# Layer 0 attention: finer side steps for channel attention and statistics, and a fifth buffer of weights in the second sample

## The chip, the cores and the metric

The kernel runs on one core of a Trainium2 chip. The metric is the device time of one launch in microseconds. Before the change it was measured in three runs: 4051.79, 4053.4 and 4055.28 us, so the median is 4053.4 us. One more execution was taken with the hardware profiler, and all durations of instructions come from it.

## What is computed

Two images x of 128 channels and 64 x 64 pixels go through four layers, each x = x + layer(groupnorm(x)). The change concerns layer 0 alone. Cut to what matters:

```python
xn = biasfree_ln(x, ln1_w)
qkv = conv1x1(xn, w_qkv)
qkv = depthwise_3x3(qkv, w_dw)                       # 5 groups of 128 channels
q1, k1, v, q2, k2 = split(qkv, 5)                    # 4 heads of 32 channels each
q1, q2, k1, k2 = map(l2norm_tokens, (q1, q2, k1, k2))
attn1 = softmax(einsum('bhnc,bhmc->bhnm', q1, k1) * temperature)   # 4096 x 4096 per head
out1 = einsum('bhnm,bhmc->bhnc', attn1, v)
attn2 = softmax(einsum('bhnc,bhnd->bhcd', q2, k2) * temperature)   # 32 x 32 per head
out2 = einsum('bhnc,bhcd->bhnd', v, attn2)
out = conv1x1(out1 + out2, w_po)
out = conv1x1(biasfree_ln(out, ln2_w), w_proj) + b_proj

def _gn(v, G=32, eps=1e-5):                          # before every layer
    m = mean(g); s = var(g)                          # over 4 channels and all pixels
    return (g - m) / sqrt(s + eps)
```

The first pair, attn1 and out1, is the token attention. The second, attn2 and out2, is called channel attention here.

## The kernel before

Layer 0 treats the two samples one after the other. For each it runs the convolutions (`convolutions`), then the attention (`attention`), and the end of the layer (`finish`), which is spread into the next sample's convolutions or runs by itself after the second sample.

`attention` is one loop of 256 iterations per sample, written out in full: 8 blocks of 512 queries (`qb`) times 32 tiles of 128 keys (`kt`). All four heads are treated in one iteration, on four groups of 32 rows of TensorE. Iteration n issues, in this order:

- the score matmuls of n (`scores`, L1850 in the profile): one head's scores into the single bank 6, three heads' into three of the banks 0 to 5, which alternate between even and odd iterations;
- the row-sum matmuls (`totals`, the same line L1842 as the multiplication), only at kt 28 and at kt 1;
- ScalarE's exponential of the single bank (L1918), a side step in every fourth iteration (n % 4 == 3), and the exponential of the three banks (L1921), both into the tile `weights` of n (128 x 4 x 512 f32, 8 KB in each partition);
- the multiplication of the weights of n-2 with the values (`multiply`, L1842), accumulated over a block;
- VectorE's addition of the weights of n (`add`, L1873, 128 x 2048), by which the row sums are collected in two interleaved series (even and odd n) and cut into shorter sums at the key tiles STARTS = (0, 1, 14, 27). At these four tiles nothing is added: the sum starts from the weights' own tile, which is then read by the addition two iterations later;
- after a row-sum matmul, ScalarE's copy of the bank to `total` (`emptied`, L1889), and in the first iterations of the next block the transposes, the reciprocal and the scaling of the block's queries by VectorE (`normalized`, L1895 to L1904, with the tile `turned`).

Inside `_in_order` every engine executes its instructions in the program's order, so an instruction that waits holds back all that follow on its engine. The tiles of `pool` (f0_p) have 4 buffers, except the three of `sums` and the single `total` and `turned`. The exponentials of iteration n overwrite the weights of n-4, so they wait for the last reader of those: TensorE's multiplication and VectorE's addition.

Side work hides beside this loop. It is written as generators, and `next(side)` runs one piece up to the next `yield`; a piece's instructions stand in the engines' queues before the second exponential and the addition of its iteration. Piece k is issued in iteration 4k-1. In the first sample `side` holds `channel_attention` (7 yields) and then `normalize` of the second sample (40 yields, among them the 11 of `_stats_steps`); in the second sample it holds `channel_attention` and `_stats_steps` for the first sample's output (the statistics that layer 1 needs). What is not done when the loop ends is run after it. PSUM for side pieces comes from `half()`, which takes one of the two banks that `at["spare"]` names: they belong to the other parity's three banks.

`channel_attention` folds the heads' products of q2 and k2 by two matmuls (L1781, 512 columns, and L1782, 8 columns, which needs the reduction L1779), copies them by ScalarE (L1786, L1788), reduces them per head (L1793, L1799), takes the norms' power -0.5 on GpSimd (`_power`, L1403 and L1404), scales, transposes and exponentiates a 128 x 32 tile (L1802 to L1810), divides (L1811, L1816) into the block-diagonal `a2`, transposes that (L1820) and multiplies it with `w_po` (L1826) into `w2`.

`xn`, the normalized input (128 x 4096 f32), is read by the convolutions. In the first sample, the second sample's `normalize` writes it anew during the attention. In the second sample nothing uses it after the convolutions.

Of the kernel before, what the change touches and what calls it, by code (L numbers as in the profile page):

```python
# [10 lines left out]
F32 = mybir.dt.float32  # L11
# [7 lines left out]
CH = 512  # L19
# [1381 lines left out]
def _power(nc, pool, out, x, least, add, exponent):  # L1401

    nc.vector.tensor_scalar(out, x, least, add, ALU.max, ALU.add)  # L1403
    nc.gpsimd.tensor_tensor(out, out, exponent.to_broadcast(list(out.shape)), ALU.pow)  # L1404


def _stats_steps(nc, pool, psum_tile, x, cst, mhalf, got, by_scalar=False):

    def taken(ps, name):
        if not by_scalar:  # L1410
            return ps[:, 0:1]
        t = pool.tile([128, 1], F32, tag=name, name=name)
        nc.scalar.copy(t, ps[:, 0:1])
        return t

    st = pool.tile([128, NCH, 6], F32, tag="gn_st", name="gn_st")
    for c in range(NCH):
        nc.vector.bn_stats(st[:, c, :], x[:, c * CH : (c + 1) * CH])
        yield
    mv = pool.tile([128, 2], F32, tag="gn_mv", name="gn_mv")  # L1420
    nc.vector.bn_aggr(mv, st)
    yield
    pm = psum_tile()
    nc.tensor.matmul(pm[:, 0:1], cst["group"], mv[:, 0:1], start=True, stop=True)
    mean = got[:, 0:1]
    nc.vector.tensor_copy(mean, taken(pm, "gn_pm"))
    d = pool.tile([128, 1], F32, tag="gn_d", name="gn_d")
    nc.vector.tensor_sub(d, mv[:, 0:1], mean)
    e = pool.tile([128, 1], F32, tag="gn_e", name="gn_e")
    nc.vector.scalar_tensor_tensor(e, d, d, mv[:, 1:2], ALU.mult, ALU.add)  # L1430
    yield
    pv = psum_tile()
    nc.tensor.matmul(pv[:, 0:1], cst["group"], e, start=True, stop=True)
    _power(nc, pool, got[:, 1:2], taken(pv, "gn_pv"), 0.0, 1e-5, mhalf)
    yield


# [11 lines left out]
def _layer0(ctx, tc, X, a, cst, worst, there, dram):  # L1449
    nc = tc.nc  # L1450
# [15 lines left out]
    def half():  # L1466
        if at["spare"] is None:
            return sp()[:, 0, :]
        return banks[:, at["spare"].pop(0), :]

    ident = cst["ident"]
    mhalf = one.tile([128, 1], F32, name="mhalf")
# [303 lines left out]
    def channel_attention(ss2, own, w2):  # L1776

        sums = small.tile([128, 2, 4], F32, tag="sums2", name="sums2")
        nc.vector.tensor_reduce(sums, ss2, AX.X, ALU.add)  # L1779
        ps, sq = half(), half()  # L1780
        nc.tensor.matmul(ps, fold.rearrange("p r i -> p (r i)"), own.rearrange("p r c -> p (r c)"), start=True, stop=True)  # L1781
        nc.tensor.matmul(  # L1782
            sq[:, :8], fold.rearrange("p r i -> p (r i)"), sums.rearrange("p n r -> p (n r)"), start=True, stop=True
        )
        folded = cp.tile([128, CH], F32, tag="gn", name="folded", bufs=1)
        nc.scalar.copy(folded, ps)  # L1786
        both = small.tile([128, 8], F32, tag="both", name="both")
        nc.scalar.copy(both, sq[:, :8])  # L1788
        gram = small.tile([128, 32], F32, tag="gram", name="gram")
        n2 = small.tile([128, 2], F32, tag="n2", name="n2")  # L1790
        for r in range(4):
            rr = slice(32 * r, 32 * r + 32)
            nc.vector.tensor_reduce(  # L1793
                gram[rr, :],
                folded[rr, r * 128 : (r + 1) * 128].rearrange("p (c q) -> p q c", c=4),
                AX.X,
                ALU.add,
            )
            nc.vector.tensor_copy(n2[rr, :], both[rr, r:8:4])  # L1799
        yield  # L1800
        _power(nc, small, n2, n2, 1e-24, 0.0, mhalf)
        nc.vector.tensor_scalar_mul(gram, gram, n2[:, 1:2])  # L1802
        lg = small.tile([128, 32], F32, tag="lg", name="lg")
        nc.vector.transpose(lg, gram)
        nc.vector.tensor_scalar(lg, lg, n2[:, 0:1], temp, ALU.mult, ALU.mult)
        nm = small.tile([128, 1], F32, tag="nm2", name="nm2")
        nc.vector.tensor_reduce(nm, lg, AX.X, ALU.max, negate=True)
        yield
        sm = small.tile([128, 1], F32, tag="sm2", name="sm2")
        nc.scalar.activation(lg, lg, AF.Exp, bias=nm, accum_out=sm)  # L1810
        nc.vector.reciprocal(sm, sm)  # L1811
        a2 = small.tile([128, 128], F32, tag="a2", name="a2", bufs=1)
        nc.gpsimd.memset(a2, 0.0)
        for h in range(4):
            hh = slice(32 * h, 32 * h + 32)
            nc.vector.tensor_scalar_mul(a2[hh, hh], lg[hh, :], sm[hh, :])  # L1816
        yield
        yield
        pt = half()
        nc.tensor.transpose(pt[:, :128], a2, ident)  # L1820
        a2t = small.tile([128, 128], F32, tag="a2t", name="a2t", bufs=1)
        nc.scalar.copy(a2t, pt[:, :128])
        yield
        yield
        pt = half()
        nc.tensor.matmul(pt[:, :128], a2t, w_po, start=True, stop=True)  # L1826
        nc.scalar.copy(w2, pt[:, :128])
        yield


    def attention(pool, side):

        sums = acc(1)
        single = banks[:, 6, :]
# [50 lines left out]
            return qb, first, bank  # L1885

        def emptied(qb, first, bank):
            t = pool.tile([128, CH], F32, tag="total", name="total", bufs=1)
            nc.scalar.copy(t, bank)  # L1889
            totalled.append((qb, first, t))  # L1890

        def normalized(qb, first, t):
            cols = slice(qb * CH, (qb + 1) * CH)
            turned = pool.tile([128, CH // 32, 32], F32, tag="turned", name="turned", bufs=1)
            nc.vector.transpose(turned.rearrange("p n i -> p (n i)"), t)  # L1895
            if first:
                by_query[qb] = small.tile([128, CH // 32], F32, tag="first", name="first")
                nc.vector.tensor_copy(by_query[qb], turned[:, :, 0])
                return
            rec = small.tile([128, CH // 32], F32, tag="rec", name="rec")  # L1900
            nc.vector.tensor_add(rec, turned[:, :, 0], by_query.pop(qb))
            nc.vector.reciprocal(rec, rec)
            nc.vector.transpose(turned, rec.unsqueeze(2).to_broadcast([128, CH // 32, 32]))
            nc.vector.tensor_mul(  # L1904
                q1[:, cols], q1[:, cols], turned.rearrange("p n i -> p (n i)")
            )

        for n in range(last + 1):
            kt = n % NQT
            mine, other = 3 * (n % 2), 3 * ((n + 1) % 2)  # L1910
            three = banks[:, mine : mine + 3, :]
            at["spare"] = [other, other + 1]
            held[n] = pool.tile([128, 4, CH], F32, tag="weights", name="weights")
            scores(n, three)
            total = None
            if len(pending) == 2 and kt in (STARTS[-1] + 1, 1):
                total = totals(banks[:, other + 2, :])
            nc.scalar.activation(held[n][:, 0, :], single, AF.Exp)  # L1918
            if n % 4 == 3:
                next(side, None)  # L1920
            nc.scalar.activation(held[n][:, 1:, :], three, AF.Exp)  # L1921
            if total:
                emptied(*total)
            if n > 1:
                multiply(n - 2)
            add(n)
            if totalled and kt < 2:
                normalized(*totalled.pop())
# [56 lines left out]
    def chain(*gens):  # L1985
        for g in gens:
            yield from g
# [31 lines left out]
    for b in range(B):  # L2019
        w2 = small.tile([128, 128], F32, tag="w2", name="w2")  # L2020
        with tc.tile_pool(name="f0_conv", reuse_waits="tile", bufs=1) as pool, _in_order(tc):
            ss2, own = convolutions(pool, b, before)
        if b == 0:

            with _after(tc):
                rows_of_weights = _weights_by_rows(nc, dram, a)
        side = [channel_attention(ss2, own, w2)]
        if b + 1 < B:
            side.append(normalize(b + 1))
        if b:  # L2030
            side.append(
                _stats_steps(
                    nc,
                    small,
                    half,
                    X[:, b - 1, :],
                    cst,
                    mhalf,
                    there[:, b - 1],
                    by_scalar=True,  # L2040
                )
            )
        with tc.tile_pool(name="f0_p", reuse_waits="tile", bufs=4) as pool, _in_order(tc):
            attention(pool, chain(*side))
        before = finish(b, w2)
    with _in_order(tc):
        run(before)
# [530 lines left out]
```

## Time and profile before

| | |
|---|---|
| median of three runs | 4053.4 us |
| profiled execution, its own time | 4055.79 us |
| its span, first to last instruction | 4054.0 us |
| TensorE busy in the span | 3872.8 us (96%) |
| VectorE busy | 3198.9 us (79%) |
| ScalarE busy | 3242.3 us (80%) |
| attention of the first sample | about 189 to 776 us |
| attention of the second sample | about 969 to 1536 us |
| TensorE, VectorE, ScalarE busy in 189 to 776 | 570.06, 541.99, 520.07 of 587 us |
| TensorE, VectorE, ScalarE busy in 969 to 1536 | 556.88, 527.66, 507.03 of 567 us |
| exponential L1918, L1921 (mean) | 0.599, 1.446 us |
| addition L1873 (mean) | 2.287 us |

A line of the timeline reads: start in us, duration in us, engine, line of the kernel, operation, output<-inputs, shapes, number of merged instructions, and in brackets the engine's idle time before it with what ended it. PE is TensorE, PEld its loading of weights, DVE is VectorE, ACT is ScalarE, POOL is GpSimd. A line of the page's group list ends with the busy time, the mean duration in ns, and the idle time of the engine just before, with what ended most of it. In the attention three engines are all busy for nine tenths of the time, so a short wait of one soon becomes a wait of another.

### The profile page before, as it was taken

To read this page: it belongs to the slowest core of one execution; us is meant where nothing else is said; L and a number is where in the kernel's file an instruction comes from. 1 tells how busy PE (TensorE), PEld (TensorE's weight loads), DVE (VectorE), ACT (ScalarE), POOL (GpSimd) and SP (SyncE) were. 2 spreads that over 40 slices of the span, in tenths; PEclk is the share of its full clock that TensorE was granted. 3 is DMA by queue.
4 is the path that set the end of the run, shared out by engine and by line. 5 is a ranking of instruction groups with operands and counts; after the bars stand their busy time and mean duration, and the time that the engine had idled before them with its cause. 6 is when DMAs were issued, how large, how long until landed. Compare 5 with 4: busy or idle time off the path is not lost.

```text
span 4054.0 us, 82178 instructions
## 1 busy us (share of the span) xinstructions
PE 3872.8 (96%) x35214; PEld 1324.0 (33%) x35214; DVE 3198.9 (79%) x3572; ACT 3242.3 (80%) x3955; POOL 90.7 (2%) x145
## 2 busy tenths in 40 slices
PE   7899999989999998997998999999999999999998
PEld 4511221244121114445665222232222322222222
DVE  5699999766999998996766787777777777776666
ACT  4489889735899993325654899999999999999998
POOL 1000000010010001000000000000000000000000
PEclk9999999999999998998998999999999999999999
DMA  1199960000000000003663110110002000110000
GB/s 50 17 197 187 185 105 2 1 2 2 2 2 2 2 2 13 6 1 150 278 259 112 53 40 27 45 55 27 27 29 73 25 27 30 39 52 6 6 6 4
DMA packets 193128, 217.59 MB, mean 54 GB/s; under 512 B 30441, under 2 KB 154345, under 8 KB 188658
## 3 DMA queue, kind: packets, MB, share of 16 engines
q1 hardware_dynamic: 192754, 212.25, 20.3%
q8 instruction: 278, 4.55, 0.5%
q14 instruction: 96, 0.79, 0.1%
HBM read 178.64 MB, written 98.57 MB: 68 GB/s over the span
## 4 chain that ended last, share of the span: by engine, by line
PE 65%; DVE 7%; ACT 2%; issue 2%; POOL 0%; SPq 0%; DMA 0%; ACTq 0%; POOLq 0%; DVEq 0%
PE ps_acc L2293 25%; PE ps_s L2270 18%; PE ps L1842 5%; PE ps L1850 5%; PE ps_bank L710 2%; DVE sums L1873 2%; PE ps_z L1008 2%; DVE e L950 2%; PE ps_t L640 1%; PE ps_bank L590 1%; PE ps_bank L681 1%; PE ps_bank L1062 1%; PE ps_acc L2151 1%; PE ps_acc L2197 1%; PE ps_pe L925 1%
## 5 line engine op out<-in xcount | busy, mean ns | idle before, releaser
L2284 ACT ACTIVATE weights<-ps_s 128x1024 f32<-128x1024 f32 x1920 | 1781.4, 1062 | 75.6 <-PE ps_s L2270 75.5
L2293 PE MATMUL ps_acc<-weights,vt 128*32 128x512 f32 x8192 | 1092.7, 605 | 0.0
L1873 DVE TENSOR_TENSOR sums<-sums,weights 128x2048 f32<-128x2048 f32 x384 | 855.3, 2287 | 15.8 <-ACT weights L1921 14.5
L2270 PE MATMUL ps_s<-q,k 64*128 64x512 f32 x4096 | 831.0, 470 | 3.7 <-DMA k<-stack 2.5
L1921 ACT ACTIVATE weights<-ps 128x1536 f32<-128x1536 f32 x512 | 740.6, 1446 | 8.9 <-PE ps L1850 8.9
L2270 PEld LDWEIGHTS ps_s<-q,k 64*128 64x128 f32 x4096 | 348.4, 184 | 935.7 <-ACT weights L2284 809.2
L1850 PE MATMUL ps<-q,k 32*64 32x512 f32 x8192 | 577.0, 615 | 21.6 <-ACT weights L1918 19.4
L1842 PE MATMUL ps<-weights,vt 128*32 128x512 f32 x4096 | 548.3, 607 | 0.0
L2242 DVE SCALAR_TENSOR_TENSOR exp_z<-exp_z,exp_m 128x1024 f32<-128x1024 f32 x384 | 469.1, 1222 | 9.3
L1918 ACT ACTIVATE weights<-ps 128x512 f32<-128x512 f32 x512 | 306.8, 599 | 107.1 <-DVE sums L1873 38.6
L2226 DVE TENSOR_SCALAR exp_i<-ps_s 128x1024 int32<-128x1024 f32 x128 | 156.8, 1225 | 216.2 <-PE ps_s L2270 216.0
L1850 PEld LDWEIGHTS ps<-q,k 32*64 32x64 f32 x8192 | 120.8, 130 | 456.4 <-ACT weights L1918 403.4
L2293 PEld LDWEIGHTS ps_acc<-weights,vt 128*32 128x32 f32 x8192 | 161.9, 108 | 309.3 <-issue 308.5
L1842 PEld LDWEIGHTS ps<-weights,vt 128*32 128x32 f32 x4096 | 84.4, 108 | 392.7 <-issue 379.4
L662 DVE SCALAR_TENSOR_TENSOR X<-g,w,X 128x2048 f32<-128x2048 f32 x84 | 197.4, 2351 | 2.6
L1873 DVE TENSOR_TENSOR sums<-weights 128x2048 f32<-128x2048 f32 x64 | 145.9, 2289 | 39.8 <-ACT weights L1921 39.3
L2246 DVE SCALAR_TENSOR_TENSOR weights<-exp_z,exp_i 128x1024 f32<-128x1024 f32 x128 | 156.8, 1225 | 15.9 <-ACT weights L2284 0.5
L2242 DVE SCALAR_TENSOR_TENSOR exp_z<-exp_m 128x1024 f32<-128x1024 f32 x128 | 156.0, 1219 | 0.0
L1008 PE MATMUL ps_z<-w_ri,e 128*32 128x128 f32 x2048 | 137.3, 408 | 14.1 <-DVE e L950 11.9
L1613 PE MATMUL ps<-pad,diag 32*32 32x512 f32 x4032 | 142.3, 604 | 4.1 <-ACT vt L1624 3.7
L1591 PE MATMUL ps<-xn,w_qkv 128*128 128x512 f32 (+1 forms) x200 | 87.3, 583 | 22.5 <-ACT pad L1598 14.1
L950 DVE TENSOR_SCALAR e<-ps_pe 32x136 f32<-32x136 f32 (+1 forms) x352 | 104.3, 296 | 4.9
(304 smaller groups left out, 2976.7 us busy)
## 6 DMA issues: line engine op xcount, KB each, us to landing
w_ri<-w_r SPq DMA_DIRECT2D x16, 2112.0 KB, 8.0
w_ri<-w_i SPq DMA_DIRECT2D x16, 2112.0 KB, 13.6
stack<-qs SPq DMA_DIRECT2D x64, 256.0 KB, 2.1
q<-stack SPq DMA_DIRECT2D x128, 128.0 KB, 2.5
k<-stack SPq DMA_DIRECT2D x128, 128.0 KB, 2.6
stack<-ks SPq DMA_DIRECT2D x32, 256.0 KB, 2.2
w_r<-in_L_conv_kr_w SPq DMA_DIRECT2D x15, 528.0 KB, 12.6
w_r<-in_L_conv_kr_x SPq DMA_DIRECT2D x15, 528.0 KB, 12.6
```

What stands on the lines that cost most here:

```text
L662: nc.vector.scalar_tensor_tensor(xi, g[:, i : i + H // 2, j : j + W], w8[:, s : s + 1], xi, ALU.mult, ALU.add)
L950: nc.vector.tensor_scalar_mul(out, got[of, :, s], sign)
L1008: nc.tensor.matmul(out.rearrange("p (n f o) -> p n f o", n=2, f=2), e[:, s, 2 * j : 2 * j + 2, :].rearrange("p f x -> p (f x)"), w.rearran ...
L1842: nc.tensor.matmul(out[rows, :], lhs(rows), w[:, j, :], start=first, stop=stop)
L1850: nc.tensor.matmul(bank[64 * h : 64 * h + 64, :], k1[rows, kt * 128 + 64 * h : kt * 128 + 64 * h + 64], q1[rows, qb * CH : (qb + 1) * CH], ...
L1873: nc.vector.tensor_add(parts[p].rearrange("p j c -> p (j c)"), t.rearrange("p j c -> p (j c)"), w.rearrange("p j c -> p (j c)"),)
L1918: nc.scalar.activation(held[n][:, 0, :], single, AF.Exp)
L1921: nc.scalar.activation(held[n][:, 1:, :], three, AF.Exp)
L2242: nc.vector.scalar_tensor_tensor(z, x, n, m, ALU.add, ALU.mult)
L2270: nc.tensor.matmul(ps[j // 2][:, j % 2, :], g.k[kt // 4][rows, j // 2, keys], g.q[qb][rows, j // 2, :], start=True, stop=True,)
L2284: nc.scalar.activation(w[0], ps[p], AF.Exp)
L2293: nc.tensor.matmul(g.ac[32 * j : 32 * j + 32, :], g.vt[:, kt, j // 2, i : i + 2, :].rearrange("p a d -> p (a d)"), w[:, i, :], start=(at = ...
```

## The change

There are two parts.

The first cuts side work into more pieces. In `channel_attention` the clearing of `a2` moves to the first piece, which otherwise keeps only the reduction L1779; a yield stands between this and the folding matmuls, one between ScalarE's copies of them and the reductions per head, one after `_power`, and one after the exponential. Two empty pieces go: the double yields before and after the transpose become single ones. It has 9 yields instead of 7. `_stats_steps` gets, for its use beside an attention (`by_scalar`), a yield after each of ScalarE's two copies out of PSUM, before VectorE reads the copy: 13 instead of 11. All that comes later in `side` is issued 2 or 4 pieces, that is 8 or 16 iterations, later.

The second part concerns the sample number b, which `attention` now gets. The tile `weights` has 4 + b buffers. In the second sample `total` and `turned` are not tiles of the pool but the first and the second 512 columns of `xn`. There is one of each, as before.

```diff
@@ _stats_steps
-    nc.vector.tensor_copy(mean, taken(pm, "gn_pm"))
+    got_mean = taken(pm, "gn_pm")
+    if by_scalar:
+        yield
+    nc.vector.tensor_copy(mean, got_mean)
...
-    _power(nc, pool, got[:, 1:2], taken(pv, "gn_pv"), 0.0, 1e-5, mhalf)
+    var = taken(pv, "gn_pv")
+    if by_scalar:
+        yield
+    _power(nc, pool, got[:, 1:2], var, 0.0, 1e-5, mhalf)
     yield
@@ channel_attention
         nc.vector.tensor_reduce(sums, ss2, AX.X, ALU.add)
+        a2 = small.tile([128, 128], F32, tag="a2", name="a2", bufs=1)
+        nc.gpsimd.memset(a2, 0.0)
+        yield
         ps, sq = half(), half()
...
         nc.scalar.copy(both, sq[:, :8])
+        yield
         gram = small.tile([128, 32], F32, tag="gram", name="gram")
...
         yield
         _power(nc, small, n2, n2, 1e-24, 0.0, mhalf)
+        yield
         nc.vector.tensor_scalar_mul(gram, gram, n2[:, 1:2])
...
         nc.scalar.activation(lg, lg, AF.Exp, bias=nm, accum_out=sm)
+        yield
         nc.vector.reciprocal(sm, sm)
-        a2 = small.tile([128, 128], F32, tag="a2", name="a2", bufs=1)
-        nc.gpsimd.memset(a2, 0.0)
         for h in range(4):
             hh = slice(32 * h, 32 * h + 32)
             nc.vector.tensor_scalar_mul(a2[hh, hh], lg[hh, :], sm[hh, :])
-        yield
         yield
         pt = half()
         nc.tensor.transpose(pt[:, :128], a2, ident)
...
         yield
-        yield
         pt = half()
@@ attention
-    def attention(pool, side):
+    def attention(pool, b, side):
...
-            t = pool.tile([128, CH], F32, tag="total", name="total", bufs=1)
+            t = xn[:, :CH]
+            if b == 0:
+                t = pool.tile([128, CH], F32, tag="total", name="total", bufs=1)
             nc.scalar.copy(t, bank)
...
-            turned = pool.tile([128, CH // 32, 32], F32, tag="turned", name="turned", bufs=1)
+            turned = xn[:, CH : 2 * CH].rearrange("p (n i) -> p n i", i=32)
+            if b == 0:
+                turned = pool.tile([128, CH // 32, 32], F32, tag="turned", name="turned", bufs=1)
...
-            held[n] = pool.tile([128, 4, CH], F32, tag="weights", name="weights")
+            held[n] = pool.tile([128, 4, CH], F32, tag="weights", name="weights", bufs=4 + b)
```

More of the change, by code (lines that the diff above doesn't have):

```diff
@@ L2043, in _layer0 @@
         with tc.tile_pool(name="f0_p", reuse_waits="tile", bufs=4) as pool, _in_order(tc):
-            attention(pool, chain(*side))
+            attention(pool, b, chain(*side))
         before = finish(b, w2)
```

## The prediction

> **What bounds the kernel now.** First the whole page, for the chain of waits and the costliest groups.
>
> ```profile
> ## 4 chain that ended last, share of the span: by engine, by line
> PE 65%; DVE 7%; ACT 2%; issue 2%; POOL 0%; SPq 0%; DMA 0%; ACTq 0%; POOLq 0%; DVEq 0%
> ...
> L1873 DVE TENSOR_TENSOR sums<-sums,weights 128x2048 f32<-128x2048 f32 x384 | 855.3, 2287 | 15.8 <-ACT weights L1921 14.5
> ...
> L1921 ACT ACTIVATE weights<-ps 128x1536 f32<-128x1536 f32 x512 | 740.6, 1446 | 8.9 <-PE ps L1850 8.9
> ...
> L1918 ACT ACTIVATE weights<-ps 128x512 f32<-128x512 f32 x512 | 306.8, 599 | 107.1 <-DVE sums L1873 38.6
> ```
>
> TensorE leads. In layer 0's attention (189 to 776 us for the first sample, 969 to 1536 for the second) ScalarE waits 38.6 us for VectorE's additions to free a buffer of weights. Then the timeline, undisturbed in the second sample:
>
> ```profile
> 1404.34 0.60 ACT L1918 ACTIVATE weights<-ps 128x512 f32<-128x512 f32 x1 [0.46 <-PE ps L1850]
> ...
> 1405.20 1.11 PE L1850 MATMUL ps<-q,k 32*64 32x512 f32 x16
> ...
> 1407.24 1.11 PE L1850 MATMUL ps<-q,k 32*64 32x512 f32 x16
> ...
> 1408.70 0.60 ACT L1918 ACTIVATE weights<-ps 128x512 f32<-128x512 f32 x1 [0.38 <-DVE sums L1873]
> ...
> 1409.35 1.12 PE L1850 MATMUL ps<-q,k 32*64 32x512 f32 x16
> ...
> 1410.72 4.49 DVE L1873 TENSOR_TENSOR sums<-sums,weights 128x2048 f32<-128x2048 f32 x2
> ```
>
> Score groups (L1850) normally start 2.04 us apart (1405.20 to 1407.24): I call this the beat. A late buffer moves the next start, 1409.35, to 2.11. And the worst place in the second sample's first block:
>
> ```profile
> 1005.36 1.11 PE L1850 MATMUL ps<-q,k 32*64 32x512 f32 x16
> ...
> 1007.03 0.60 ACT L1918 ACTIVATE weights<-ps 128x512 f32<-128x512 f32 x1 [0.65 <-DVE sums L1873]
> ...
> 1016.31 0.60 ACT L1918 ACTIVATE weights<-ps 128x512 f32<-128x512 f32 x1 [2.94 <-DVE sums L1873]
> ...
> 1016.96 1.50 PE L1850 MATMUL ps<-q,k 32*64 32x512 f32 x16 [2.76 <-ACT weights L1918]
> ...
> 1018.79 1.94 PE L1842 MATMUL ps<-weights,vt 128*32 128x512 f32 x8
> ```
>
> VectorE is late by a side step, ScalarE waits 2.94 us for its buffer, TensorE idles 2.76 us; afterwards the multiply takes 1.94 us instead of 1.06.
>
> **The skill.** "TensorE: Matmul & The Clock Gate", Part 1 (the HAM clock gate), says that an idle stretch puts TensorE at half clock for a window of about 3.4 us. The trace agrees: its clock record is 0.5 from 1017.57 to 1020.99 (3.42 us), and likewise from 201.79, 239.33 and 580.67 in the first sample. The same page (Architectural detail) calls ScalarE and VectorE strict FIFO: what stands behind a waiting instruction waits too, as the additions here do. "Perfetto Trace Analysis", Optimization Strategy, says that repeated equal bubbles can mean too few buffers; here ScalarE waits for a buffer four times in every undisturbed block.
>
> **The rule that I carry.** Let an iteration's score group start at P. From the timeline: L1918 starts at P+1.18, the next score group keeps the beat while L1918 starts by P+1.39, and the weights can be added at P+3.2. Additions follow each other at 2.21 (22.11 us for ten), so each makes VectorE 0.17 later against the beat; I call the delay of an addition's start its lateness. Key tiles 0, 1, 14 and 27 of a block have no addition, which gives back 2.04. An ordinary buffer is free 5.5 plus lateness after its P. But tile 14's weights are only read by tile 16's addition. With four buffers tile 18 wants them at P(16)+5.47, so tile 16 may have no lateness; with five, tile 19 wants them, and 2.0 is allowed (ordinary tiles: 4.1 and 6.1). Row sums on TensorE at tiles 28 and 1 add 1.75 each and set a second deadline that buffers don't move: tile 25's addition may be 2.5 late, tile 31's 0.5. Undisturbed, the rule gives losses of 0.07 and 0.17 at tiles 4 and 5 and some 0.2 at 18; the trace has 0.07, 0.16 and 0.17.
>
> **Part by part, second sample (five buffers).** Losses are distances of score groups beyond 2.04 (beyond 3.79 with row sums), from the timeline.
> - Fold step. Before, at iteration 3, TensorE waits between two fold matmuls for a reduction that stands behind a 2.29 addition: the distance is 5.27, loss 3.23. After, the reduction is issued one step earlier; at iteration 7 the folds' own time stays: two passes of 0.53 and about 0.3 for the small one, 1.40 (the ScalarE copies of 0.59 and 0.17 end before the next bank is due). Gain 1.8.
> - VectorE pieces. Before: 1.95 at iteration 7 (992.62 to 994.57, 0.82 of it waiting for GpSimd's power) and 1.27 at 11; losses 0.28+0.16+0.17+2.84 at 15 to 18, and the half clock adds 1.4 (1.66+0.12 less the transpose's own 0.40). Together 4.85. After: 2.05 at 11 (four reductions and copies), 0.16 at 15, 0.95 at 19 (no wait for the power), 1.27 at 27. Carried: the folds clear the lateness at 8; 0.5+2.05 at 11; 2.9 at 13; 2.90+2.21-4.08+0.16=1.2 at 15; 1.4 at 16, under 2.0: nothing lost there. 2.8 at 19, 3.84 at 25: 1.3 over 2.5, lost at tile 28. Gain 3.5. This is what is late next.
> - Statistics. Eight bn_stats (0.61 each between additions) stand at tiles 31, 3, 7 ... 27 before; they lose 0.33 at tile 1, 0.07 and 0.76 at 4 and 5, 1.68 at 18: 2.84. After, they begin at tile 7 of the second block: lateness 1.0 at 7, 2.3 at 11, 1.55 at 16 (allowed), 4.3 at 25: 1.8 lost at tile 28. Gain 1.0. Third block: 1.36 before, 1.43 after (the mean's and variance's matmuls keep 0.40 each; splitting their copies from them hides behind VectorE, which is late anyway, and would gain at most 0.2).
> - Steady buffer waits of the last five blocks: 0.75, three times 0.47, 0.46: gain 2.6, with nothing late next, since lateness 2.0 at 25 is under 2.5.
> - Row sums' temporaries in the input: the same instructions at other addresses, one buffer each as before; the input's last reader, the convolution, ended before 969. I cost it at nothing, bounds 0 and +2 (the copy of 0.59 waiting for a late transpose in the three disturbed blocks).
>
> Sum: -1.8-3.5-1.0+0.1-2.6 = -8.8.
>
> **First sample (four buffers).** Fold step: 3.70 and 0.81 (half clock) before; 1.40 and an undisturbed 0.40 after: -2.7. Pieces: 3.18 at 15 to 18 and 1.66 of half clock before; 1.4 at 18 after (lateness 1.4, none allowed): -3.4. Statistics in the second block: 2.84 before, 1.6 at tile 18 and 0.3 of row sums after: -0.9. Then the next sample's normalization, four steps, 16 iterations, later. Its ScalarE pieces (0.59 to 0.81) and transposes (0.61 per step on TensorE) keep their price. The seven long VectorE steps (2.05: spread and scaling) move from tiles 7, 19, 31, 11, 23, 3, 11 to 23, 3, 15, 27, 7, 19, 27. Before, the one at tile 3 collided: 2.02 lost and 1.5 of half clock after it (580.67). After, again only tile 3's does, carried at 1.9, and the last ones cost 1.7 at tiles 28 to 5 of the sixth and seventh block. Blocks three to seven: 367.0 before, 365.6 carried: -1.4. There are 52 beats, 106 us, behind the last step, so the steps still end inside the loop. Sum: -8.4.
>
> Five stalls of 1.3 to 1.9 remain. Before, 1.68 (twice) drew no half clock, 2.02, 2.56 and 2.84 did. I allow for one, +1.4. The memset on GpSimd (0.20) is hidden; no DMA is moved. Total -8.8-8.4+1.4 = -15.8. The profiled execution took 4055.8 with a span of 4054.0, so the span after is 4038.2; from the runs' median of 4053.4 I get 4037.6.
>
> **Rivals.** A measurement of this kernel can tell about 0.2%, 8.1 us, from no change.
> - Half clock returns: all five stalls draw a window, four more than counted, +5.6: 4043. For: TensorE's margin between 1.68 and 2.02 is thin. Against: two of 1.68 were harmless.
> - The fifth buffer does not do what it says: if accesses to the input tile are ordered as a whole, or lateness is caught at the row sums anyway, the second sample behaves as with four buffers (1.4 at 18, 1.6, and the steady 2.6 stays): +4.5: 4042. Against: the tile already is used in separate columns by the normalization.
> - Slower: the normalization's long steps, moved by half a block, collide with the tight tiles in the four-buffer sample. A collision costs what iteration 165 shows, 2.0 and 1.5 of half clock, 3.5. From five more the gain is gone; if all seven others of the eight (the first lasts 1.36) collide, seven times 3.5, +24.5: 4062.1. For: one of them did collide before. Against: between them TensorE loses 0.6 per four beats, in which VectorE catches up.
>
> **Numbers.** Forecast 0.62, half clock 0.18, fifth buffer 0.10, slower 0.05; 0.05 for no change by anything else. Of the first, nearly all is below 4045.3; of the second and third about three quarters: faster 0.81, same 0.13, slower 0.06. The range reaches 6.6 down (no half clock, no stall at tile 28 or collision) to 4031 and up past the two middle cases to 4047.
>
> **What would show it.** Second sample: no ScalarE wait for an addition in the last five blocks (17.8 us over the sample before), blocks of 68.8 instead of 69.25; no 2.9 us wait at iteration 18, but TensorE waiting about 1.3 and 1.8 us for additions at the row sums of the first two blocks. First sample: about 1.4 at iteration 18. Both: fold matmuls back to back at iteration 7, about 1.4. Wrong would be a stall of over 2 us at iteration 18 of the second sample, longer blocks where normalization now ends, or a different distance from the attention's end to layer 1.

## The result

| | before | after |
|---|---|---|
| median time, us | 4052.6 (4046.74 to 4055.28) | 4034.34 (4028.9 to 4041.58) |
| span of the profiled execution, us | 4054.0 | 4027.1 |
| ahead of the first sample's attention | 197.7 | 190.1 |
| attention of the first sample | 576.96 | 568.74 |
| between the attentions | 202.9 | 203.0 |
| attention of the second sample | 556.08 | 546.05 |
| what follows | 2520.3 | 2519.2 |

Six runs of each kernel were timed, so the median of before stands a little below the 4053.4 of the first three. The changed kernel is faster: ratio 0.9957, 95% interval 0.9944 to 0.9971, 18.3 us between the medians. The lower rows cut each profile at score groups: an attention here is the distance from the fourth to the last of its 256. The two attentions became 18.2 us shorter. The 7.6 us ahead of them come from unchanged code and are not the change's: the changed kernel, profiled again, began its attention at 193.7, and the experiment *Temporaries only* below, whose code up to there is that of before, at 191.3.

Views of the changed kernel are read in the order of the prediction. The page's chain of waits by engine, and its groups (the score groups are now L1858, the multiplications and row sums L1850, the exponentials L1930 and L1933, the addition L1881):

```profile
PE 68%; DVE 5%; issue 2%; ACT 1%; POOL 0%; SPq 0%; DMA 0%; POOLq 0%; DVEq 0%; ACTq 0%
...
L1881 DVE TENSOR_TENSOR sums<-sums,weights 128x2048 f32<-128x2048 f32 x384 | 854.9, 2285 | 7.8 <-ACT weights L1933 5.6
...
L1933 ACT ACTIVATE weights<-ps 128x1536 f32<-128x1536 f32 x512 | 740.7, 1447 | 8.5 <-PE ps L1858 8.5
...
L1930 ACT ACTIVATE weights<-ps 128x512 f32<-128x512 f32 x512 | 306.6, 599 | 88.3 <-PE ps L1858 33.5
```

None of the instructions shown became shorter by more than 0.1%. What changed is who waits: TensorE's share of the chain rose from 65 to 68%, and the idle time ahead of the first exponential, of which the largest part ended with an addition before (38.6 us), now with a score group (33.5). The view of waits for the second sample's attention (waiting engine and line, what it waited for, us in all, times, longest), one row of before and then two of the changed kernel:

```profile
ACT weights L1918 <- DVE sums L1873: 17.4, 31, 2.9
```

```profile
ACT weights L1930 <- PE ps L1858: 18.8, 42, 1.3
...
PE ps L1850 <- DVE sums L1881: 2.3, 2, 1.4
```

ScalarE's wait for an addition is gone. In its place TensorE waits twice for an addition itself, at the row sums. The timeline of TensorE shows the first of these, at tile 28:

```profile
1014.07 1.11 PE L1858 MATMUL ps<-q,k 32*64 32x512 f32 x16
1015.14 1.06 PE L1850 MATMUL ps<-sums,ones 128*32 128x512 f32 x8
1017.10 1.07 PE L1850 MATMUL ps<-sums,ones 128*32 128x512 f32 x8 [0.89 <-DVE sums L1881]
1017.98 1.04 PE L1850 MATMUL ps<-weights,vt 128*32 128x512 f32 x8
1018.95 1.11 PE L1858 MATMUL ps<-q,k 32*64 32x512 f32 x16
```

The row sums' first half reads a sum that was ready. The second half needs the series' last addition and starts 1.96 us after the first instead of 0.9. The distance of the score groups is 4.88, 1.09 over the 3.79 that this place takes without a wait.

The fold step, in the first sample:

```profile
198.73 1.12 PE L1858 MATMUL ps<-q,k 32*64 32x512 f32 x16
...
200.08 1.13 PE L1790 MATMUL ps<-own,fold 128*128 128x512 f32 x2 [0.22 <-ACT weights L1933]
...
201.04 0.28 PE L1791 MATMUL ps<-sums,fold 128*128 128x8 f32 x2
...
201.25 1.07 PE L1850 MATMUL ps<-weights,vt 128*32 128x512 f32 x8
...
202.25 0.69 PE L1858 MATMUL ps<-q,k 32*64 32x512 f32 x8
```

The reduction was issued a step before, so the small fold follows the large one without a gap; 198.73 to 202.25 is 3.52, 1.48 over the beat. And an undisturbed block of the second sample:

```profile
1382.32 1.11 PE L1858 MATMUL ps<-q,k 32*64 32x512 f32 x16
...
1383.50 0.60 ACT L1930 ACTIVATE weights<-ps 128x512 f32<-128x512 f32 x1
...
1384.36 1.11 PE L1858 MATMUL ps<-q,k 32*64 32x512 f32 x16
...
1385.48 0.60 ACT L1930 ACTIVATE weights<-ps 128x512 f32<-128x512 f32 x1
...
1386.40 1.11 PE L1858 MATMUL ps<-q,k 32*64 32x512 f32 x16
```

Every score group is 2.04 after the last, and no exponential has a wait in brackets. Last, the busy time in one stretch per attention (stretch; busy us and instructions of TensorE, its weight loads, VectorE, ScalarE, GpSimd; granted clock; DMA share; GB/s), before and after:

```profile
198.00:775.00 577.00, 561.27 (x6371) 114.68 (x6363) 539.08 (x384) 514.95 (x559) 22.25 (x11) 0.99 0.71 121
979.00:1535.00 556.00, 547.11 (x6303) 107.73 (x6306) 524.75 (x304) 500.44 (x534) 16.60 (x3) 1.00 0.01 2
```

```profile
190.00:759.00 569.00, 556.79 (x6375) 114.93 (x6379) 538.61 (x384) 514.94 (x559) 15.82 (x11) 1.00 0.73 122
963.00:1510.00 547.00, 544.55 (x6311) 107.84 (x6315) 524.99 (x304) 503.44 (x536) 11.93 (x2) 1.00 0.01 2
```

VectorE and ScalarE do the same work as before (the second stretch after has two instructions of ScalarE more at its edges). TensorE is busy for 4.5 us less in the first sample. The three half-clock windows of before, half of three times 3.42 or 5.1, are of that size, and the clock record has none inside either attention of the changed kernel.

### The profile page after: what moved, and what is told of

The parts are those of the page before. It is cut to its first block, busy times and chain, and to the rows that moved or that the text cites. A ratio compares the mean times of both kernels' runs of the same rounds, so it can differ in the third digit from the quotient of the medians.

```text
span 4027.1 us, 82181 instructions
## 1 busy us (share of the span) xinstructions
PE 3855.3 (96%) x35214; PEld 1323.1 (33%) x35214; DVE 3198.8 (79%) x3572; ACT 3242.4 (81%) x3955; POOL 79.5 (2%) x145
## 4 chain that ended last, share of the span: by engine, by line
PE 68%; DVE 5%; issue 2%; ACT 1%; POOL 0%; SPq 0%; DMA 0%; POOLq 0%; DVEq 0%; ACTq 0%
PE ps_acc L2305 25%; PE ps_s L2282 18%; PE ps L1850 6%; PE ps L1858 6%; PE ps_bank L710 2%; PE ps_z L1008 2%; DVE e L950 2%; PE ps_t L640 1%; PE ps_bank L590 1%; PE ps_bank L1062 1%; PE ps_bank L681 1%; PE ps_acc L2209 1%; PE ps_acc L2163 1%; PE ps_pe L925 1%; DVE sums L1881 1%
## 5 line engine op out<-in xcount | busy, mean ns | idle before, releaser
L1881 DVE TENSOR_TENSOR sums<-sums,weights 128x2048 f32<-128x2048 f32 x384 | 854.9, 2285 | 7.8 <-ACT weights L1933 5.6
L1933 ACT ACTIVATE weights<-ps 128x1536 f32<-128x1536 f32 x512 | 740.7, 1447 | 8.5 <-PE ps L1858 8.5
L1858 PE MATMUL ps<-q,k 32*64 32x512 f32 x8192 | 575.0, 613 | 12.5 <-ACT weights L1930 11.8
L1850 PE MATMUL ps<-weights,vt 128*32 128x512 f32 x4096 | 545.0, 604 | 0.0
L1930 ACT ACTIVATE weights<-ps 128x512 f32<-128x512 f32 x512 | 306.6, 599 | 88.3 <-PE ps L1858 33.5
L1858 PEld LDWEIGHTS ps<-q,k 32*64 32x64 f32 x8192 | 120.6, 130 | 442.5 <-ACT weights L1930 393.4
L1850 PEld LDWEIGHTS ps<-weights,vt 128*32 128x32 f32 x4096 | 84.5, 108 | 391.1 <-issue 378.1
L1881 DVE TENSOR_TENSOR sums<-weights 128x2048 f32<-128x2048 f32 x64 | 145.8, 2289 | 32.7 <-ACT weights L1933 31.9
L1619 PEld LDWEIGHTS ps<-pad,diag 32*32 32x32 f32 x4032 | 84.3, 104 | 59.3 <-issue 21.4
```

Of the source, the lines that this page charges most:

```text
L1619: nc.tensor.matmul(ps[r // 2][to, r % 2, :].rearrange("p (h w) -> p h w", w=W), diag[rows, grp, t, :], pad[rows, y0 : y0 + ROWS, t % 3 : t ...
L1850: nc.tensor.matmul(out[rows, :], lhs(rows), w[:, j, :], start=first, stop=stop)
L1858: nc.tensor.matmul(bank[64 * h : 64 * h + 64, :], k1[rows, kt * 128 + 64 * h : kt * 128 + 64 * h + 64], q1[rows, qb * CH : (qb + 1) * CH], ...
L1881: nc.vector.tensor_add(parts[p].rearrange("p j c -> p (j c)"), t.rearrange("p j c -> p (j c)"), w.rearrange("p j c -> p (j c)"),)
```

## The experiments

The theory is the rule that the prediction carries from tile to tile: VectorE's lateness costs time only at a deadline, and there are two kinds, the weights' buffers and the row sums. The rivals are that the gain has another source (the temporaries, the cut of the statistics, missing half clock) and that more buffers would have bought the same or more. "First sample" and "second sample" below mean their attentions, measured as in the table. The cuts in channel attention were not undone one by one: what the fold, the power and the exponential gained each is read from the timelines and was not tested apart.

**Buffers only.** Before, with the second part of the change and none of the first; of the edit only the buffers' line is shown, and the temporaries move as in the change.

```diff
-            held[n] = pool.tile([128, 4, CH], F32, tag="weights", name="weights")
+            held[n] = pool.tile([128, 4, CH], F32, tag="weights", name="weights", bufs=4 + b)
...
```

> The kernel before with the second part of the change alone: five buffers of weights and the row sums' temporaries in the input in the second sample, side pieces as before. Theory (lateness of VectorE against two kinds of deadline): the second sample's distance from the fourth score group to the last, 556.1 before, falls to about 550: the 3.2 at iteration 3 stays, the wait of 2.9 at iteration 18 and the steady waits go, and some 0.6 and 2.0 of stall appear at the row sums of tile 28 in the first two blocks. First sample unchanged at 577. In all about -6 against before, a little more than half of it from the removed stalls. Rival A (the buffers do nothing but take the steady waits): -2.6. Rival B (the gain of the second sample is all the buffers'): -10.

Measured: 4043.06 us, ratio to before 0.9978 (0.9969 to 0.9987); second sample 548.77, 7.3 less than before, of which some 1.4 are a half-clock window that did not come. That lies between the two rivals' 2.6 and 10. The first sample, whose code is that of before, took 573.86 and not the expected 577; the section on the prediction comes back to it. The long wait at tile 18 was expected to go; it is shorter, not gone. Its timeline:

```profile
1010.24 0.60 ACT L1922 ACTIVATE weights<-ps 128x512 f32<-128x512 f32 x1 [1.50 <-DVE sums L1873]
...
1010.89 1.26 PE L1850 MATMUL ps<-q,k 32*64 32x512 f32 x16 [0.75 <-ACT weights L1922]
```

ScalarE waits 1.50 where it waited 2.94, and TensorE 0.75 where it waited 2.76, now one tile later; at the row sums of tile 28 in the first and second block another 0.28 and 2.06 are lost. The steady blocks are already at 68.77.

**Steps only.** The changed kernel with four buffers in both samples.

```diff
-            held[n] = pool.tile([128, 4, CH], F32, tag="weights", name="weights", bufs=4 + b)
+            held[n] = pool.tile([128, 4, CH], F32, tag="weights", name="weights", bufs=4)
```

> The changed kernel with four buffers of weights in both samples (the temporaries stay in the input). Theory: the first sample is as in the changed kernel, 568.7; the second one's distance is about 551.8 instead of 546.1, with a stall of about 1.4 at iteration 18, 1.6 at tile 18 of the second block and the steady waits of 0.4 to 0.5 per block back. In all 5 to 6 slower than the changed kernel, some 12 to 13 faster than before. Rival A (fifth buffer of no use but for the steady waits): 2.6 slower than the changed kernel. Rival B (the second sample's gain is the buffer's alone): 10 slower.

Measured: 4036.69, ratio 0.9970 (0.9958 to 0.9981); second sample 550.95, first 568.80. ScalarE's line in the view of waits, second sample:

```profile
ACT weights L1930 <- DVE sums L1881: 15.3, 29, 1.9
```

The waits are back (17.4 us in before); tile 18 loses 1.31 in the first block and 1.53 in the second. The fifth buffer is worth 4.9 on top of the steps, so the rival that it does nothing has fallen. In the second sample steps alone give 5.1 and buffers alone 7.3, both together 10.0: they partly remove the same waits, and the half-clock window behind tile 18, worth some 1.4, is missing in each of the three. The medians show less than the attentions, 2.4 us between this kernel and the changed one, which is below what the stages around the attentions vary by.

**Temporaries only.** Before, with `total` and `turned` of the second sample in `xn`, no fifth buffer and no new steps.

```diff
-            t = pool.tile([128, CH], F32, tag="total", name="total", bufs=1)
+            t = xn[:, :CH]
+            if b == 0:
+                t = pool.tile([128, CH], F32, tag="total", name="total", bufs=1)
...
```

> The kernel before with nothing but the row sums' temporaries moved into the input in the second sample. Theory: the same instructions and the same waits, so 577.0 and 556.1 stay and the time is that of before within noise; also a look at how far the part ahead of the attention (fourth score group at 197.8 in the profile before, 190.1 after, though nothing there was changed) moves by itself. Rival (accesses to the input are ordered as a whole): up to 2 slower, in the blocks where VectorE is late at tile 1.

Measured: 4048.71, ratio 1.0001 (0.9993 to 1.0009); second sample 556.45. The move costs and gains nothing; it only makes room.

**Row sums two tiles later.** The changed kernel, first row sums at tile 30 instead of 28.

```diff
-            if len(pending) == 2 and kt in (STARTS[-1] + 1, 1):
+            if len(pending) == 2 and kt in (STARTS[-1] + 3, 1):
```

> The changed kernel with the first row-sum matmuls of each block at key tile 30 instead of 28. It separates two readings of the stalls of 1.1 and 1.6 at tile 28 in the second sample. Theory (VectorE has more to add than TensorE's beat allows in these blocks; the row sums are only where it shows): the stalls at 28 go, but about as much comes back at the row sums of tile 1 and at tile 3 to 6, so the second sample stays within 1 of 546.1. Rival (the deadline at 28 is the only cause): 2.7 faster.

Measured: 4025.08, ratio 0.9939 (0.9926 to 0.9953); second sample 545.84, first 566.30. In the second sample TensorE's timeline has the row sums of tile 30 in one piece and the wait at those of tile 1:

```profile
1026.35 1.92 PE L1850 MATMUL ps<-sums,ones 128*32 128x512 f32 x16
...
1034.48 1.06 PE L1850 MATMUL ps<-sums,ones 128*32 128x512 f32 x8
1036.37 1.07 PE L1850 MATMUL ps<-sums,ones 128*32 128x512 f32 x8 [0.82 <-DVE sums L1881]
```

The deadline was put off, VectorE's arrears were not: 2.69 are no longer lost at tile 28 of the first two blocks, but 1.03 and 1.86, formerly under 0.06 and 0.34, at tile 1 of the blocks that follow. The second sample stays within 0.2 of the changed kernel's, as the theory had it, so the rival that the deadline at 28 is the only cause has fallen. The first sample gained 2.4, which the rule did not say. The median lies 9.3 below the changed kernel's, but the attentions account for only 2.7 of that; the rest is not explained, and the profiled execution took 4033.1.

**The changed kernel again**, no edit.

> The changed kernel once more, beside the others of this call. Attention as in its profile: 568.7 and 546.1 us from the fourth score group to the last. The part ahead of it, where the two first profiles differ by 7.6 us (197.7 and 190.1) with no change in the code, should land anywhere between these: then those 7.6 us of the first pair of profiles belong to no change. If it is again at 190, the change does reach the part ahead of the attention.

Measured: 4034.8, ratio 0.9962 (0.9949 to 0.9975); attentions 568.79 and 546.07, within 0.05 of the first profile, while the span is 4035.3 against 4027.1. An attention without half-clock windows repeats to a few hundredths; the stages around it do not.

**Six buffers.** The changed kernel, in the second sample every sixth iteration's weights in the free half of the input.

```diff
+            if b and n % 6 == 5:
+                held[n] = xn[:, 4 * CH :].rearrange("p (j c) -> p j c", j=4)
+            else:
                 held[n] = pool.tile([128, 4, CH], F32, tag="weights", name="weights", bufs=4 + b)
```

> The changed kernel with a sixth buffer of weights in the second sample, placed in the second half of the free input. Theory: with five no buffer is waited for any more, and what is left (1.1 at tile 28 of the first block, 1.6 of the second) is VectorE's lateness at the row sums, which buffers don't move: 546.1 stays within 0.3. Rival (the stalls at the row sums still come from buffers): 1 to 3 faster.

Measured: 4034.88, ratio 0.9967 (0.9956 to 0.9977); second sample 545.94 against 546.05. The same stall as with five, on TensorE's timeline:

```profile
1023.58 1.06 PE L1850 MATMUL ps<-sums,ones 128*32 128x512 f32 x8
1025.54 1.07 PE L1850 MATMUL ps<-sums,ones 128*32 128x512 f32 x8 [0.90 <-DVE sums L1881]
```

What is left in the second sample is not a matter of buffers; the deadline that holds there after the change is the row sums'.

**Five buffers in both samples.** The pool has no room for five buffers and both temporaries, so in the first sample `total` lies in `own`, whose last readers are the fold matmuls, and `turned` in the last columns of `xn` until normalization reaches them, then in a tile that is free there.

```diff
-                t = pool.tile([128, CH], F32, tag="total", name="total", bufs=1)
+                t = own.rearrange("p r c -> p (r c)")
...
-                turned = pool.tile([128, CH // 32, 32], F32, tag="turned", name="turned", bufs=1)
+                at_end = xn[:, 7 * CH :]
+                if qb >= 6:
+                    if late[0] is None:
+                        late[0] = cp.tile([128, 4, C], F32, tag="y", name="late_turned")
+                    at_end = late[0].rearrange("p t c -> p (t c)")
+                turned = at_end.rearrange("p (n i) -> p n i", i=32)
...
-            held[n] = pool.tile([128, 4, CH], F32, tag="weights", name="weights", bufs=4 + b)
+            held[n] = pool.tile([128, 4, CH], F32, tag="weights", name="weights", bufs=5)
```

> The changed kernel with five buffers in the first sample too; the row sums' temporaries of that sample lie in a small tile that is free after the folds and in the input's last columns, for the last two blocks in a tile of the finished normalization. Theory: the wait at iteration 18, those at tile 18 of the following blocks and the collision at iteration 133 go, smaller stalls at row sums appear: the first sample falls from 568.7 to about 562, the second stays at 546.1; 7 faster than the changed kernel. Rival (VectorE's work is the bound in these blocks, a buffer only shifts where it shows): under 2 faster.

Measured: 4027.19, ratio 0.9945 (0.9933 to 0.9957), 7.6 less than the changed kernel's 4034.8 beside it; first sample 559.71, 9.0 less than the changed kernel, where 6.7 were expected. ScalarE's longest row of waits in that attention:

```profile
ACT weights L1936 <- PE ps L1859: 17.8, 38, 1.3
```

In the changed kernel the longest row there is 18.8 us in 26 waits for additions. Normalization's pieces, which make VectorE late in the first six blocks, mostly meet no deadline now.

**All together.** Five buffers in both, the later row sums, and in the second sample a side step in every eighth iteration.

```diff
-            if n % 4 == 3:
+            if n % (4 + 4 * b) == 3 + 4 * b:
```

> Five buffers in both samples, the first row sums of a block at key tile 30, and the second sample's side pieces at every eighth iteration instead of every fourth. Theory: carried with the same rule, first sample about 562, second about 545; with what the later row sums showed before (2.4 in the first sample) perhaps 560. In all 8 to 10 faster than the changed kernel, 25 faster than before. Rival (side pieces at wider distance meet the tight tiles more often): second sample over 547, no faster than five buffers in both alone.

Measured: 4021.68, ratio 0.9937 (0.9924 to 0.995), with 4034.8 for the changed kernel beside it; attentions 558.73 and 543.83. It is the fastest version that was run; its attentions are 12.3 us shorter than the changed kernel's, its time 13.1, against 8 to 10 expected. The wider side steps were not run alone: the second sample is 2.0 shorter here than with the later row sums alone, and that they are the cause is likely, not shown.

**Statistics unsplit.** The changed kernel without the two new yields of `_stats_steps`.

```diff
-    if by_scalar:
-        yield
...
```

> The changed kernel without the two new yields in the statistics: the copies out of PSUM and VectorE's reading of them stand in one piece again, and what follows is issued two pieces, 8 iterations, earlier. Theory: the splits themselves hide nothing that costs, since VectorE is later than ScalarE's copy anyway: second sample 546 within 0.3. In the first sample the normalization lands on other tiles; carried, its blocks come out 0.8 shorter: 568 instead of 568.7, with the collision moved from iteration 133 to others. Rival (VectorE's wait for the copies was worth something): second sample 0.4 or more longer.

Measured: 4033.71, one run, with 4043.16 for one run of before beside it: too few to say more of the time; second sample 546.05, as with the cut; first 567.25 against 568.74. The cut as such is worth nothing in the second sample. Its effect in the first is to shift normalization by two pieces, which changed the collisions there (the losses at iterations 114 and 161 replaced others) by 1.5.

## Why the prediction was right

Forecast 4037.6, measured 4034.34: inside the range and on the forecast side. Two small slips in its working change nothing: ten additions in 22.11 us include the whole 2.29 of the last, so they follow each other at 2.20 and not 2.21; and the terms named for the lower end of the range (1.4, 1.3, 1.8 and 1.9) add up to 6.4 and not 6.6. Its terms, beside the same distances in the profile after:

| term | forecast | measured |
|---|---|---|
| fold step left, second sample | 1.40 | 1.20 |
| lost at tile 28, first block | 1.3 | 1.09 |
| lost at tile 28, second block | 1.8 | 1.60 |
| steady waits of the last five blocks, gain | 2.6 | 2.6 |
| third block | +0.07 | -0.36 |
| second sample, sum | -8.8 | -10.0 |
| lost at tile 18, first and second block, first sample | 1.4 and 1.6 | 1.32 and 1.53 |
| normalization's collision at tile 5 of the fifth block | 1.9 | 1.81 |
| blocks three to seven, first sample | 365.6 | 366.0 |
| first sample, sum | -8.4 | -8.2 |
| half clock | +1.4 | 0 |

- *Which wait is late next* was right, and steps-only and six-buffers show it from both sides: without the fifth buffer the loss is at tile 18, with it at the row sums, and a sixth changes nothing.
- *Temporaries at nothing* was right: 1.0001. *Splitting the statistics' copies gains at most 0.2* was right: 0.00 in the second sample.
- *The slower rival* (seven more collisions in normalization, at 3.5 each) did not come: there was the one that was carried, where it was put, and without half clock. *The fifth buffer does nothing* was wrong by 4.9.
- *The half clock* is the step that was wrong in kind, and it is a term of the sum. The prediction took it for a matter of length: idle stretches that lost 1.68 were harmless, those of 2.02 and more drew a window. The first sample of before shows otherwise, beside the buffers-only run, whose first sample has the same code. TensorE's timeline at the fold step and at tile 18, in before and then in buffers-only:

```profile
201.35 0.39 PE L1782 MATMUL ps<-sums,fold 128*128 128x8 f32 x2 [1.35 <-DVE sums L1779]
201.67 1.88 PE L1842 MATMUL ps<-weights,vt 128*32 128x512 f32 x8
...
238.08 1.12 PE L1850 MATMUL ps<-q,k 32*64 32x512 f32 x16 [2.49 <-ACT weights L1918]
```

```profile
197.13 0.39 PE L1782 MATMUL ps<-sums,fold 128*128 128x8 f32 x2 [1.35 <-DVE sums L1779]
197.45 1.06 PE L1842 MATMUL ps<-weights,vt 128*32 128x512 f32 x8
...
232.21 1.12 PE L1850 MATMUL ps<-q,k 32*64 32x512 f32 x16 [2.48 <-ACT weights L1922]
```

The idle times are the same, 1.35 at the fold step and 2.49 against 2.48 at tile 18. Before has a window right after each of them (from 201.79 and 239.33; the multiplication after the fold takes 1.88), buffers-only after neither (the multiplication takes its usual 1.06). Temporaries-only has the same two idle times and no window after them either. Buffers-only and temporaries-only both have one window in this attention (at 572.2 and 570.5), which answers to the one at 580.67 of before, but before has three, and their attentions take 573.86 and 573.85 against 576.96.

The Trainium skill, "TensorE: Matmul & The Clock Gate", Part 1 (the HAM clock gate), says of the warm-up that the activity window is free-running, and that the same kernel therefore measures differently from run to run. The records agree: the windows of before inside the attentions begin at 201.79, 239.33, 580.67 and 1017.57, which are 11, 100 and 128 times 3.413 apart, and in all eleven profiles here the starts of the windows of one execution lie whole multiples of 3.413 apart, to within 0.01 us. Where the same idle time falls on this grid makes the difference at tile 18. Busy time of TensorE in the stretches of the grid that hold it, one in before, two in buffers-only (stretch; its length; busy us and instructions; granted clock; DMA share; GB/s):

```profile
235.92:239.33 3.41, 1.12 (x16) 1.00 1.24 202
```

```profile
227.42:230.83 3.41, 2.22 (x28) 1.00 1.26 190
230.83:234.24 3.41, 1.76 (x21) 1.00 1.26 212
```

In before 2.16 of the idle 2.49 us fall into one stretch and the next is at half clock; in buffers-only, as in temporaries-only (1.72 and 2.36), a border of the grid divides it. The other windows inside an attention, in any of the profiles, follow stretches in which TensorE was busy for 0.65 to 1.47 us, and no stretch there with 1.68 or more was followed by one, with a single exception: the one at 201.79 follows a stretch of 2.04, and the same idle time at the fold step of temporaries-only, also with 2.04 in its stretch, drew none. What decided there stays open. The table in the same Part 1, which the prediction draws on, lets the clock drop after an idle window of about 3.4 us; no stretch ahead of these windows was idle throughout, and the measurement decides.

So 3.1 of the first sample's 8.2 were in the profile of before and not in its code, and that the forecast of 8.4 agrees with 8.2 is to that extent luck: both count from the same profile. By the other two executions of that code, the change takes 5.1 from the first sample. With the second sample's 10.0 (where temporaries-only, too, has the window of before) that makes 15.1, against 18.3 between the medians, whose interval is 11.8 to 22.7 (0.29 and 0.56% of 4052.6). When the changed kernel was timed again, its median lay 14.0 below that of before beside it (4048.82). Which of these is nearer the mean gain stays open, because it needs the windows of many executions and the timed runs have no clock record at this grain. That none of the changed kernel's stalls, up to 1.81, drew a window in any profile here is an observation; that none can was not shown.

## What to carry to other kernels

List every deadline that an engine's lateness can miss, not only the buffers: a further buffer is worth what it takes from the first deadline, up to the next one, which it does not move (here a fifth gave 4.9 us and a sixth 0.1). Cut a side step where one engine waits inside it for another with work queued behind; a cut in front of an engine that is late anyway gained nothing here (the statistics, 0.00). And where buffers do bind, look for memory that is free for just this stage, in each sample by itself: the same fifth buffer gave 4.9 us in the second sample and 9.0 in the first.

## What had not been expected

- Five buffers in the first sample gave 9.0 us instead of 6.7, and later row sums gave 2.4 there but 0.2 in the second sample. In the first sample normalization's steps keep VectorE late for six blocks; the 2.4 are spread over these blocks (0.5, 0.5 and 0.6 in the fourth to sixth), and which steps they belong to was not taken apart.
- The part ahead of the first attention, the same code in all these kernels, ended between 190.1 and 197.7 us in the profiles here. Its half-clock windows lie differently each time: in before 6.8 us from 68.7 and one each at 109.6, 147.2 and 184.7, after only three, at 100.7, 138.3 and 162.2. A single pair of spans here is therefore no measure of a change below some 8 us, while an attention without half-clock windows repeats to 0.05.
